# A routed layer's results: gathered and summed by the next stage, or added to the tokens' rows in HBM by DMA

## The chip, the cores and the metric

The kernel runs on one core of a Trainium2 chip. The metric is the device time of one execution in microseconds (us). The engines are PE (TensorE matmul; PEld are its weight loads), DVE (VectorE), ACT (ScalarE), POOL (GpSimd) and SP (SyncE, which here only issues DMAs). Each runs its own instructions in order and waits on semaphores for the others. A DMA is issued by an engine's queue and carried out by 16 DMA engines that all queues share.

## The reference

Four layers follow each other on 4096 tokens of 256 float32 numbers, each as `x = x + norm(layer(norm(x)))`: a windowed attention, a routed layer of experts, a second (linear, causal) attention, and a gated recurrence. The change is about the hand-over from the second to the third. The routed layer is

```python
scores = softmax(xt @ gate_w.T)                  # 8 experts
topk_w, topk_i = top_k(scores, 2)                # 2 of them for each token
comb = zeros((T, 8)).at[arange(T)[:, None], topk_i].add(topk_w)
for e in range(8):
    y = y + comb[:, e:e+1] * ((silu(xt @ w1[e]) * (xt @ w3[e])) @ w2[e])   # 256 -> 704 -> 256
y = y + (silu(x @ sw1) * (x @ sw3)) @ sw2        # shared expert, 256 -> 384 -> 256
```

and what follows is `x = x + norm(y)`, then `norm(x)` into the second attention.

## The kernel before

The tokens are 32 tiles of 128 rows, or 16 units of two tiles; a tile of x has the tokens on the 128 partitions. All arithmetic is float32.

**Stage A (0 to about 350 us): first attention, routing, most of the shared expert.** Units pass through a pipeline written out by hand: `ORDER_A` lists pieces with a lag each, and every engine executes its part in that order. When a unit is through, its normed rows lie in the SBUF tile `xrow`. `rank` computes both experts of each token, their weights (`wts`) and a slot for each copy; `send` (L835) scatters every tile of `xrow` twice, by indirect DMA from POOL, to the slots in the HBM tensor `xg_d`, which has one region for each expert. `zeros` (L862) first fills the ends of the regions with zeros (8 DMAs from SP). The last eight sends wait for these fills. The shared expert's result of units 0 to 12 goes to the HBM tensor `ysh_d`.

**Stage B (about 358 to 877 us): experts.** The rows of `xg_d` are handled in 32 blocks of 256 rows and 4 blocks of 128 (which expert a block belongs to is computed at run time; 4 more blocks stand in a branch that runs only if needed). For each block: `x_rows` (L1184, SP) loads its rows two blocks ahead, `x_cols` transposes them, `up` does the two wide products (L1211), `angle_piece` computes a part of the third layer's rotation table on DVE (into `xrow`, whose rows have been sent), and `down` of the block before (L1248, L1255) does the product back to 256 columns. `down` copies its result from PSUM to `yo` (DVE, L1258) and SP stores it at the block's place in the HBM tensor `yg_d` (L1260). Weights of the next block (2 MB) are loaded by SP meanwhile. `place_results` computes for each token where in `yg_d` its two results lie (`yslots`).

**The passage.** After the branch (L1331) SP loads the second attention's weights (`second_weights`, L1031 to L1046), and PE does the shared expert of units 13 to 15 (`shared`, L1131 and L1144), whose results SP stores to `ysh_d` (L1155), and a small product of gate weights (`gate_product`, L1351 and L1356).

**Stage C (to about 1250 us): second attention.** Again a pipeline by hand, `ORDER_C`, over 16 units; a pair `("s0", 0)` is the piece `s0` with a lag of 0 periods. What a unit passes through first is what the change is about:

```python
fy   # SP: y = the unit's rows of ysh_d (shared result); the tile k_y has 3 buffers
g0..g3  # POOL: indirect DMA, rows of yg_d by yslots -> k_g (first and second expert, two tiles)   L334
s0, s1  # DVE: y += wts * k_g, four times a unit                                                 L348
bo_st, bo_pw, bo_nr, bo_ap, bo_ad   # norm of y (DVE, POOL, DVE, ACT), then x += y on POOL (L361)
cn_st, cn_pw, cn_nr, cn_ap          # norm of x, into y again
xt, xc, qk, sq, vz, v, z, rk, rq, tk, tq, ck, cq, pe, et, ps, pn, ...    # the attention itself
```

`_st` are the statistics, `_pw` the power of -1/2 on POOL (L301), `_nr` the shift on DVE (L307), `_ap` the application on ACT (L314). In the trace: `c_xt` is the transpose of the normed unit (xt), `c_pqk` and `c_pvz` the projections, `c_sq` ACT's silu of them, `c_kn` the rotation on POOL, `c_qr` on DVE, `c_pe` the products of keys and queries, `c_et` their masking on DVE, `c_pn` the products with the values, `c_tk` the transpose of the keys. `c_tk`, `c_xt` and the projections share two PSUM buffers, which ACT's copies free; the piece v frees that of `c_pvz`.

**Stage D (to the end): recurrence**, two steps over 8 pairs of units. The change leaves it as it is.

Of the kernel before, what the change touches and what calls it, by code (L numbers as in the profile page):

```python
# [16 lines left out]
P = 128  # L17
D = 256
NT = 32
NU = 16  # L20
NBLK = 8
E = 8
# [47 lines left out]
    ("z1", 2), ("v1", 2), ("cn_st", 1), ("tk1", 2), ("os1", 3), ("co_st", 4), ("g3", 0),  # L70
    ("cq1", 2), ("pn0", 3), ("ps", 2), ("tk0", 2), ("ck1", 2), ("cn_pw", 1), ("cn_nr", 1),
    ("os0", 3), ("cn_ap", 1), ("g1", 0), ("po", 3), ("co_pw", 4), ("g2", 0), ("ck0", 2),
    ("xt", 1), ("dl", 2), ("sd", 2), ("co_nr", 4), ("xc", 1), ("gt", 3), ("pe1", 2), ("tq0", 2),
    ("g0", 0), ("co_ap", 4), ("qk0", 1), ("ci_st", 3), ("et13", 2), ("cq0", 2), ("qk1", 1),
    ("ci_pw", 3), ("et12", 2), ("et10", 2), ("et11", 2), ("s1", 0), ("sq0", 1), ("s0", 0),
# [63 lines left out]
def kernel(  # L139
# [122 lines left out]
    xg_d = dram.tile([NS, D], F32, name="xg_d")  # L262
    yg_d = dram.tile([NL * BS + NM * SS, D], F32, name="yg_d")
    ysh_d = dram.tile([NT * P, D], F32, name="ysh_d")
# [3 lines left out]
    wts = [const.tile([P, NT], F32, name=f"wt{i}") for i in range(2)]  # L268
    slots = [const.tile([P, NT], I32, name=f"slot{i}") for i in range(2)]
    yslots = [const.tile([P, NT], I32, name=f"yslot{i}") for i in range(2)]  # L270
# [8 lines left out]

# [50 lines left out]
    @piece(0, 1, 2, 3)  # L330
    def g(u, n):
        t, i = n // 2, n % 2
        rows = kb.tile([P, D], F32, name=f"k_g{u}_{n}", tag="k_g", bufs=6)
        nc.gpsimd.indirect_dma_start(  # L334
            out=rows,
            out_offset=None,
            in_=yg_d[:, :],
            in_offset=bass.IndirectOffsetOnAxis(
                ap=yslots[i][:, 2 * u + t : 2 * u + t + 1], axis=0
            ),  # L340
        )
        S2[u]["g", n] = rows

    @piece(0, 1)
    def s(u, t):
        y = S2[u]["y"]
        for i in range(2):
            nc.vector.scalar_tensor_tensor(  # L348
                y[:, t, :], S2[u]["g", 2 * t + i], wts[i][:, 2 * u + t : 2 * u + t + 1],
                y[:, t, :], ALU.mult, ALU.add,  # L350
            )

# [6 lines left out]
    def bo_ad(u):  # L359
# [5 lines left out]

    xrow = const.tile([P, NT, D], F32, name="xrow")
    table = [
        xrow[:, 2 * j : 2 * j + 2, :].rearrange("p a b -> p (a b)") for j in range(NT // 2)
    ]
# [7 lines left out]
    moves = xtp.tile([P, 3, E], F32, name="rt_moves")  # L377
# [3 lines left out]
    row0 = const.tile([P, NB], I32, name="row0")  # L381
    n_small = const.tile([P, 1], I32, name="n_small")
# [4 lines left out]
    with ExitStack() as ph:  # L387
# [30 lines left out]
        def rows_of(u):  # L418
            return xrow[:, 2 * u : 2 * u + 2, :]
# [287 lines left out]
        zero = wp.tile([P, D], F32, name="zero")  # L707
        apart = wp.tile([P, 1], F32, name="apart")

        def later_constants():  # L710
            for f in range(4):
                nc.sync.dma_start(
                    out=th_d[f], in_=theta.rearrange("(i s d) f -> f s i d", i=4, s=2)[f, 0]
                )
            for vb in vbds[1:]:
                nc.gpsimd.memset(vb, 0.0)
            nc.gpsimd.memset(zero, 0.0)
            nc.sync.dma_start(
                out=xg_d[E * REG : NS, :].rearrange("(p r) d -> p r d", p=P),
                in_=zero.unsqueeze(1).to_broadcast([P, BS // P, D]),  # L720
            )
            r0 = NL * BS + NS_ALWAYS * SS
            nc.sync.dma_start(
                out=yg_d[r0:, :].rearrange("(t p) d -> p t d", p=P),
                in_=zero.unsqueeze(1).to_broadcast([P, NM - NS_ALWAYS, D]),
            )
            for dst, step, base in ((prio, -1, E), (region, REG, 0), (bidx, 1, 0)):
                nc.gpsimd.iota(
                    dst, pattern=[[step, dst.shape[1]]], base=base, channel_multiplier=0,
                    allow_small_or_imprecise_dtypes=True,  # L730
                )

            nc.gpsimd.memset(before, 1.0)
            nc.gpsimd.affine_select(
                out=before, in_=before, compare_op=ALU.is_ge, fill=0.0, base=-1,
                pattern=[[1, P]], channel_multiplier=-1,
            )
            nc.gpsimd.memset(ones, 1.0)

            nc.gpsimd.memset(seen, 0.0)  # L740
# [4 lines left out]
        def rank(g):  # L745
# [32 lines left out]
            def best(src, m, eq, nm):  # L778
                nc.vector.tensor_reduce(m, src, AX.X, ALU.max)
                nc.vector.tensor_tensor(eq, src, wide(m), ALU.is_equal)  # L780
                nc.vector.tensor_tensor(eq, eq, per_tile(prio), ALU.mult)
                q = col(f"rt_q{nm}")
                nc.vector.tensor_reduce(q, eq, AX.X, ALU.max)
                nc.vector.tensor_tensor(eq, eq, wide(q), ALU.is_equal)

            one, two = (pick[:, ts, :] for pick in picks)
            best(sc, wts[0][:, ts], one, "a")
# [3 lines left out]
            best(rest, wts[1][:, ts], two, "b")  # L791
# [41 lines left out]
        def send(t, i):  # L833

            dma = nc.gpsimd.indirect_dma_start(  # L835
                out=xg_d[:, :],
                out_offset=bass.IndirectOffsetOnAxis(ap=slots[i][:, t : t + 1], axis=0),
                in_=xrow[:, t, :],
                in_offset=None,
            )  # L840
            sent_to_rows(dma, "dispatch" if t < 2 * NZ else "last")
# [6 lines left out]
        def zeros():  # L848
# [7 lines left out]
            for e in range(E):  # L856
# [7 lines left out]
                    in_=zero.unsqueeze(1).to_broadcast([P, rows // P, D]),  # L864
# [3 lines left out]
        def blocks():  # L868
# [48 lines left out]
            nc.vector.tensor_copy(owner[:, 0:NL], of[:, 0:NL])  # L917
            yield
# [41 lines left out]
            for k, dst in ((0, row0), (1, owner)):  # L960
# [5 lines left out]
            yield  # L966


            to_big, to_few = moves[:, 0, :], moves[:, 1, :]
            nc.vector.tensor_copy(moves[:, 2, :], start)  # L970
            nc.vector.tensor_tensor(to_big, end, big, ALU.subtract)
            nc.vector.scalar_tensor_tensor(
                to_big, to_big, float(BS), region, ALU.mult, ALU.subtract
            )
            nc.vector.tensor_tensor(to_few, few_end, few, ALU.subtract)
            nc.vector.tensor_scalar(to_few, to_few, extra, float(SS), ALU.add, ALU.mult)
            nc.vector.tensor_scalar(to_few, to_few, float(NL * BS), None, ALU.add)
            nc.vector.tensor_tensor(to_few, to_few, start, ALU.subtract)
            nc.vector.tensor_tensor(to_few, to_few, to_big, ALU.subtract)
# [101 lines left out]
    with ExitStack() as ph:  # L1081
# [15 lines left out]
        def angle_piece(i):  # L1097
# [20 lines left out]
            if i % 8 == 7:  # L1118
                done = xrow[:, i - 7 : i + 1, :]
                nc.scalar.activation(done, done, AF.Sin)  # L1120
# [3 lines left out]
        def shared_part(u, c, H):  # L1124
# [16 lines left out]
            for t in range(2):  # L1141
# [6 lines left out]
                y = kb.tile([P, D], F32, name=f"k_sh{u}_{t}", tag="k_g", bufs=6)  # L1148
# [3 lines left out]
        def shared_out(u, H):  # L1152
            for t in range(2):
                r0 = (2 * u + t) * P
                nc.sync.dma_start(out=ysh_d[r0 : r0 + P, :], in_=H[3, t])  # L1155

        def place_results():

            own = yp.tile([P, NT, E], F32, name="rt_mine")
            for i, pick in enumerate(picks):  # L1160
                got = yp.tile([P, 3, NT], F32, name=f"rt_got{i}")
                for k in range(3):
                    nc.vector.tensor_tensor(
                        own, pick, moves[:, k, :].unsqueeze(1).to_broadcast([P, NT, E]),
                        ALU.mult,
                    )
                    nc.vector.tensor_reduce(got[:, k, :], own, AX.X, ALU.add)
                nc.vector.tensor_tensor(got[:, 2, :], sfs[i], got[:, 2, :], ALU.is_ge)
                nc.vector.tensor_tensor(got[:, 2, :], got[:, 2, :], got[:, 1, :], ALU.mult)
                nc.vector.tensor_tensor(got[:, 0, :], got[:, 0, :], got[:, 2, :], ALU.add)  # L1170
                nc.vector.tensor_tensor(yslots[i], got[:, 0, :], sfs[i], ALU.add)
# [9 lines left out]
        def x_rows(b, nt, at=None):  # L1181
            at = row_of(b) if at is None else at
            xg = hp.tile([P, 2, D], F32, name=f"xg{b}", tag="row", bufs=6)
# [57 lines left out]
        def down(b, nt, wb, hs):  # L1241
# [14 lines left out]
            yo = hp.tile([P, 2, D], F32, name=f"yo{b}", tag="row", bufs=6)  # L1256
            for t in range(nt):
                nc.vector.tensor_copy(yo[:, t, :], pds[t])  # L1258
            r0 = b * BS if b < NL else NL * BS + (b - NL) * SS
            nc.sync.dma_start(  # L1260
                out=yg_d[r0 : r0 + nt * P, :].rearrange("(t p) d -> p t d", p=P),
                in_=yo[:, 0:nt, :],
            )
# [32 lines left out]
        for i in range(len(line)):  # L1296
# [17 lines left out]
            if i == 32:  # L1314
                place_results()
# [4 lines left out]
            pending = (*line[i], wbs[i], hs)  # L1320
# [10 lines left out]
        with tc.If(used > NS_ALWAYS):  # L1331
            for b in range(NL + NS_ALWAYS, NB):
                ev = expert_of(b)
                wa, wb = load_up(b, ev, wa_s), load_down(b, ev, wb_s)
                down(b, 1, wb, up(b, 1, wa, x_cols(b, 1, x_rows(b, 1))))
# [33 lines left out]
        until("g3")  # L1369
        wl, wm, kview = second_weights()  # L1370
        for c in range(4):
            shared(0, c)
        until("bo_st")
# [33 lines left out]
    with ExitStack() as ph:  # L1407
# [254 lines left out]
        def spare(i):  # L1662
            return xrow[:, 2 * i : 2 * i + 2, :]
# [314 lines left out]
```

## Time and profile before

| | us |
|---|---|
| median of 3 runs | 1445.25 (1445.15 to 1445.68) |
| the profiled execution: its own time | 1430.9 |
| its span, from the first to the last instruction | 1428.7 |
| PE busy / PEld busy | 1358.0 / 1106.0 |
| DVE / ACT / POOL busy | 914.4 / 584.1 / 518.0 |
| mean granted TensorE clock | 0.985 |
| gathers k_g on POOL, x64 | 63.7 (996 ns each) |
| weighted sums k_y on DVE, x64 | 57.6 (918 ns each) |

Busy time counts an engine's instructions; matmuls are pipelined and their ends modelled, so a busy PE is not PE at its peak. "PEclk" is the clock granted to TensorE as a share of the full one. In a row of the timeline the brackets say how long the engine sat idle before and what released it, inferred from semaphores. All durations used below come from the one profiled execution, whose time is 14.35 us under the median of the runs.

### The profile page before, as it was taken

What the parts mean: (1) busy time and instruction counts of PE and PEld (TensorE: products, weight loads), DVE (VectorE), ACT (ScalarE), POOL (GpSimd) and SP (SyncE); (2) the same over time, 40 slices, a digit from 0 to 9 for tenths busy, and PEclk for the clock granted to TensorE, in tenths of its full rate; (3) what the DMA queues carried; (4) which work ended last, traced back from release to release, by engine and by line L of the source; (5) the groups of instructions that cost most, each with busy time, mean ns of one, the idle gap of its engine ahead of it and who ended that gap; (6) DMA issues with size and microseconds to landing.
All of it is one profiled execution on the core that took longest, in us unless ns stands there. A gap on an engine that the chain in (4) does not pass through costs nothing. (4 is left out here: it accounts for less than half of the span.)

```text
span 1428.7 us, 27868 instructions
## 1 busy us (share of the span) xinstructions
PE 1358.0 (95%) x10550; PEld 1106.0 (77%) x10550; DVE 914.4 (64%) x2552; ACT 584.1 (41%) x1292; POOL 518.0 (36%) x663
## 2 busy tenths in 40 slices
PE   6999999997999999999999999899999999999996
PEld 5888888875788888888888887566666666788885
DVE  6879789877445454554454542489888898535435
ACT  5776666642221222221222221344545455344443
POOL 3435666656000000000000001468788877324333
PEclk9999999998999999999999999999999999899998
DMA  8000111118554756475656465411111110000001
GB/s 203 9 9 24 45 35 46 61 38 284 182 198 155 229 174 209 152 229 164 207 187 208 162 198 138 150 32 38 46 46 45 29 33 16 2 1 29 16 31 44
DMA packets 122553, 146.60 MB, mean 103 GB/s; under 512 B 27168, under 2 KB 99632, under 8 KB 122416
## 3 DMA queue, kind: packets, MB, share of 16 engines
q1 hardware_dynamic: 115456, 126.94, 28.2%
q0 software_dynamic: 6144, 16.79, 3.8%
q8 instruction: 85, 1.39, 0.4%
q10 hardware_dynamic: 816, 1.06, 0.2%
q14 instruction: 52, 0.43, 0.1%
HBM read 113.03 MB, written 31.72 MB: 101 GB/s over the span
## 5 line engine op out<-in xcount | busy, mean ns | idle before, releaser
L1211 PE MATMUL pg<-xgT,wa 128*128 128x256 f32 (+1 forms) x1440 | 306.2, 372 | 1.9 <-ACT xgT L1200 1.8
L1211 PEld LDWEIGHTS pg<-xgT,wa 128*128 128x128 f32 x1440 | 260.0, 191 | 46.4 <-issue 11.3
L334 POOL DMA_INDIRECT k_g<-yg_d,yslot x64 | 63.7, 996 | 540.1 <-SPq L1331 526.3
L1218 DVE TENSOR_TENSOR h<-sg,pg 128x256 f32<-128x256 f32 (+1 forms) x180 | 72.9, 406 | 218.3 <-ACT sg L1216 218.3
L1216 ACT ACTIVATE sg<-pg 128x256 f32<-128x256 f32 (+1 forms) x180 | 66.7, 371 | 355.6 <-PE pg L1211 355.6
L1248 PE MATMUL pd<-wb,h 128*128 128x256 f32 x680 | 152.8, 379 | 0.0
L1248 PEld LDWEIGHTS pd<-wb,h 128*128 128x128 f32 x680 | 126.4, 190 | 16.0 <-issue 0.3
L547 POOL TENSOR_TENSOR a_pn<-a_p,a_ri 128x512 f32<-128x512 f32 x64 | 66.7, 1045 | 79.5 <-DVE a_ri L541 48.4
L1543 DVE TENSOR_TENSOR c_et<-c_pe,causal 128x512 f32<-128x512 f32 x128 | 79.2, 679 | 1.9 <-PE c_pe L1533 1.9
L835 POOL DMA_INDIRECT xg_d<-xrow,slot x64 | 65.0, 1015 | 21.1 <-issue 9.4
L656 PE MATMUL a_sh<-xnT,was 128*128 128x256 f32 x288 | 70.8, 390 | 0.0
L1810 PE MATMUL d_pg<-d_xT,wl 128*128 128x256 f32 x288 | 70.2, 379 | 0.0
L1436 PE MATMUL c_pvz<-wl,c_xT 128*128 128x512 f32 x128 | 61.5, 604 | 0.0
L656 PEld LDWEIGHTS a_sh<-xnT,was 128*128 128x128 f32 x288 | 55.1, 195 | 8.3
L1810 PEld LDWEIGHTS d_pg<-d_xT,wl 128*128 128x128 f32 x288 | 54.6, 190 | 7.6 <-ACT d_gt L1816 0.2
L348 DVE SCALAR_TENSOR_TENSOR k_y<-k_g,wt,k_y 128x256 f32<-128x256 f32 x64 | 57.6, 918 | 3.4 <-DMA k_g<-yg_d,yslot 2.3
L1436 PE MATMUL c_pqk<-wl,c_xT 128*128 128x512 f32 x128 | 57.9, 594 | 1.4 <-ACT c_qT L1514 0.7
L520 DVE TENSOR_REDUCE a_mx<-a_s 128x8 f32<-128x512 f32 x64 | 42.7, 683 | 13.5 <-PE a_s L510 12.9
L1477 POOL TENSOR_TENSOR c_kn<-c_sq,xrow 128x512 f32<-128x512 f32 x32 | 44.7, 1396 | 17.6 <-ACT c_sq L1449 17.0
L1607 PE MATMUL c_pn<-c_et,c_v 128*32 128x128 f32 x1024 | 46.8, 277 | 2.5 <-DVE c_et L1543 0.9
L1607 PEld LDWEIGHTS c_pn<-c_et,c_v 128*32 128x32 f32 x1024 | 31.0, 109 | 21.1 <-issue 14.1
L1533 PEld LDWEIGHTS c_pe<-c_qT,c_kT 32*128 32x128 f32 x1024 | 33.3, 191 | 15.1 <-issue 12.4
(320 smaller groups left out, 2834.5 us busy)
## 6 DMA issues: line engine op xcount, KB each, us to landing
wa<-in_w_dram SPq DMA_DIRECT2D x36, 704.0 KB, 5.3
wa<-in_w_dram SPq DMA_DIRECT2D x36, 640.0 KB
wb<-in_w_dram SPq DMA_DIRECT2D x36, 640.0 KB, 4.7
xg<-xg_d SPq DMA_DIRECT2D x32, 256.0 KB, 6.0
yg_d<-yo SPq DMA_DIRECT2D x32, 256.0 KB, 2.2
xg_d<-zero SPq DMA_DIRECT2D x8, 640.0 KB, 10.4
wb<-in_w_dram SPq DMA_DIRECT2D x72, 64.0 KB, 4.3
x<-in_x_dram SPq DMA_DIRECT2D x16, 256.0 KB, 5.6
```

The lines of the kernel that those rows point to most:

```text
L334: nc.gpsimd.indirect_dma_start(out=rows, out_offset=None, in_=yg_d[:, :], in_offset=bass.IndirectOffsetOnAxis(ap=yslots[i][:, 2 * u + t : ...
L547: nc.gpsimd.tensor_tensor(to, S[u].pop(("p", g)), S[u].pop(("ri", g)).unsqueeze(2).to_broadcast([P, 8, 64]), ALU.mult,)
L656: nc.tensor.matmul(to[:, i, :], ws_up[:, k, col0 : col0 + P], turned(b)[:, k, :], start=(k == 0), stop=(k == 1),)
L835: dma = nc.gpsimd.indirect_dma_start(out=xg_d[:, :], out_offset=bass.IndirectOffsetOnAxis(ap=slots[i][:, t : t + 1], axis=0), in_=xrow[:, ...
L1211: nc.tensor.matmul(pg[:, i, 0:n], wa[:, k, col0 : col0 + P], xt[:, k, 0:n], start=(k == 0), stop=(k == 1),)
L1216: nc.scalar.activation(sg[:, 0:n], pg[:, 0, 0:n], AF.Silu)
L1218: nc.vector.tensor_tensor(h[:, 0:n], sg[:, 0:n], pg[:, 1, 0:n], ALU.mult)
L1248: nc.tensor.matmul(pds[t], hs[c][:, t * P : (t + 1) * P], wb[:, c, :], start=(c == 0), stop=False,)
L1436: nc.tensor.matmul(pq, S2[u]["xT"][:, k, t * P : (t + 1) * P], w[:, k, :], start=(k == 0), stop=(k == 1),)
L1543: nc.vector.tensor_tensor(masked, S2[u]["pe", t][i], causal.unsqueeze(1).to_broadcast([P, 4, P]), ALU.mult,)
L1607: nc.tensor.matmul(out_t[32 * c : 32 * c + 32, h, :], lhs, rhs, start=(step == 0), stop=(step == last),)
L1810: nc.tensor.matmul(pg[:, m, :], a, r, start=(i == 0), stop=(i == len(prods) - 1))
```

## The change

The rows in `xg_d` become 260 numbers wide: 256 of the token, its two weights, a number that tells its first expert, and the index of its row (as an integer). `xrow` holds them in that width, `best` writes weights and the expert's number there directly, and two iota instructions write the row indices (rows of zeros point at a spare tile at the end of `ysh_d`). `down` computes each row's weight for the block's expert from them with three small DVE operations, scales the result by it where it leaves PSUM, and adds it, tile by tile, to the rows of `ysh_d` by an indirect DMA with an add, from POOL. Such a DMA names all of `ysh_d` as its target, so each waits for the one before. The pieces g and s, `yg_d`, `yslots`, `place_results` and the last part of `blocks` (`rt_moves`) are gone. `ysh_d` is set to zero for units 13 to 15, and their shared results are added by DMA from POOL instead of stored by SP. Order of instructions: on SP the first two loads of y come after `second_weights`, and no stores of `yo` are left; on POOL the adds of the shared results stand between the pieces of the first units (those of unit 14 after bo_pw and before bo_ad of the first); PE's order does not change.

```diff
+XW = D + 4
...
-    ("z1", 2), ("v1", 2), ("cn_st", 1), ("tk1", 2), ("os1", 3), ("co_st", 4), ("g3", 0),
+    ("z1", 2), ("v1", 2), ("cn_st", 1), ("tk1", 2), ("os1", 3), ("co_st", 4), 
...   # likewise g0, g1, g2, s0 and s1 taken out of ORDER_C, nothing else moved
-    xg_d = dram.tile([NS, D], F32, name="xg_d")
-    yg_d = dram.tile([NL * BS + NM * SS, D], F32, name="yg_d")
-    ysh_d = dram.tile([NT * P, D], F32, name="ysh_d")
+    xg_d = dram.tile([NS, XW], F32, name="xg_d")
+    ysh_d = dram.tile([(NT + 1) * P, D], F32, name="ysh_d")
...
-    xrow = const.tile([P, NT, D], F32, name="xrow")
+    xrow = const.tile([P, NT * XW], F32, name="xrow")
+    sent = xrow.rearrange("p (t c) -> p t c", c=XW)
+    table = [xrow[:, 2 * D * j : 2 * D * (j + 1)] for j in range(NT // 2)]
...
+            nc.gpsimd.iota(
+                zero[:, D + 3 : XW].bitcast(I32), pattern=[[0, 1]], base=NT * P,
+                channel_multiplier=1,
+            )
+            nc.gpsimd.iota(
+                sent[:, :, D + 3].bitcast(I32), pattern=[[P, NT]], base=0, channel_multiplier=1
+            )
...
             nc.sync.dma_start(
-                out=yg_d[r0:, :].rearrange("(t p) d -> p t d", p=P),
-                in_=zero.unsqueeze(1).to_broadcast([P, NM - NS_ALWAYS, D]),
+                out=ysh_d[NSD * 256 :, :].rearrange("(t p) d -> p t d", p=P),
+                in_=zero[:, 0:D].unsqueeze(1).to_broadcast([P, NT + 1 - 2 * NSD, D]),
             )
...
-            best(sc, wts[0][:, ts], one, "a")
+            best(sc, sent[:, ts, D], one, sent[:, ts, D + 2])
...
-            best(rest, wts[1][:, ts], two, "b")
+            best(rest, sent[:, ts, D + 1], two, col("rt_q"))
...
-                in_=xrow[:, t, :],
+                in_=sent[:, t, :],
...
-                    in_=zero.unsqueeze(1).to_broadcast([P, rows // P, D]),
+                    in_=zero.unsqueeze(1).to_broadcast([P, rows // P, XW]),
...
+            nc.vector.tensor_scalar(key[:, 0:NL], of[:, 0:NL], -1.0, float(E), ALU.mult, ALU.add)
...
-                y = kb.tile([P, D], F32, name=f"k_sh{u}_{t}", tag="k_g", bufs=6)
+                y = kb.tile([P, D], F32, name=f"k_sh{u}_{t}", tag="k_g", bufs=4)
...
-                nc.sync.dma_start(out=ysh_d[r0 : r0 + P, :], in_=H[3, t])
+                if u < NSD:
+                    nc.sync.dma_start(out=rows, in_=H[3, t])
+                else:
+                    nc.gpsimd.dma_start(out=rows, in_=H[3, t], accum_op=ALU.add)
...
-            xg = hp.tile([P, 2, D], F32, name=f"xg{b}", tag="row", bufs=6)
+            xg = hp.tile([P, 2, XW], F32, name=f"xg{b}", tag="xg", bufs=5)
...
-        def down(b, nt, wb, hs):
+        def down(b, nt, wb, hs, xg):
+            ws = hp.tile([P, 3, 2], F32, name=f"rt_w{b}", tag="rt_w")
+            for i, op in enumerate((ALU.is_equal, ALU.not_equal)):
+                nc.vector.scalar_tensor_tensor(
+                    ws[:, i, 0:nt], xg[:, 0:nt, D + 2], key[:, b : b + 1], xg[:, 0:nt, D + i],
+                    op, ALU.mult,
+                )
+            nc.vector.tensor_tensor(ws[:, 2, 0:nt], ws[:, 0, 0:nt], ws[:, 1, 0:nt], ALU.add)
...
-            yo = hp.tile([P, 2, D], F32, name=f"yo{b}", tag="row", bufs=6)
             for t in range(nt):
-                nc.vector.tensor_copy(yo[:, t, :], pds[t])
-            r0 = b * BS if b < NL else NL * BS + (b - NL) * SS
-            nc.sync.dma_start(
-                out=yg_d[r0 : r0 + nt * P, :].rearrange("(t p) d -> p t d", p=P),
-                in_=yo[:, 0:nt, :],
-            )
+                yo = hp.tile([P, D], F32, name=f"yo{b}_{t}", tag="yo", bufs=5)
+                nc.vector.tensor_scalar(yo, pds[t], ws[:, 2, t : t + 1], None, ALU.mult)
+                nc.gpsimd.indirect_dma_start(
+                    out=ysh_d[:, :],
+                    out_offset=bass.IndirectOffsetOnAxis(
+                        ap=xg[:, t, D + 3 : XW].bitcast(I32), axis=0
+                    ),
+                    in_=yo,
+                    in_offset=None,
+                    compute_op=ALU.add,
+                )
...
-            if i == 32:
-                place_results()
...
-        until("g3")
         wl, wm, kview = second_weights()
+        until("bo_st")
         for c in range(4):
             shared(0, c)
-        until("bo_st")
```

## The prediction

> **What bounds the kernel now.** I first read the busy time of each engine by stage (columns: stretch; its length; busy time and count of PE, PEld, DVE, ACT, POOL; granted clock; DMA share; GB/s).
>
> ```profile
> 320.00:358.00 38.00, 27.40 (x115) 21.56 (x115) 27.98 (x138) 7.99 (x17) 23.05 (x43) 0.87 0.82 267
> 358.00:877.00 519.00, 517.42 (x2532) 438.43 (x2532) 250.26 (x688) 121.37 (x324) 0.00 (x0) 1.00 0.58 188
> 877.00:911.00 34.00, 28.98 (x118) 23.25 (x118) 11.07 (x33) 6.23 (x15) 10.60 (x12) 0.90 0.51 118
> 924.00:1204.00 280.00, 263.37 (x3042) 177.60 (x3042) 247.94 (x584) 137.46 (x290) 217.88 (x242) 1.00 0.14 39
> ```
>
> The experts (358 to 877) are bound by PE: POOL does nothing there and DVE half. The second attention (924 to 1204) has DVE, POOL and PE all near full, so the sums say little; the waits must. Its c_xt starts lie 20.07 us apart, one period per unit. This is the timeline of one period, by engine (start, length, [idle before, releaser]):
>
> ```profile
> 1047.46 3.91 DVE L348 SCALAR_TENSOR_TENSOR k_y<-k_g,wt,k_y 128x256 f32<-128x256 f32 x4
> 1052.61 0.17 DVE L296 TENSOR_SCALAR ve_bo<-mv_bo 128x2 f32<-128x2 f32 x1
> ...
> 1049.30 1.28 POOL L1477 TENSOR_TENSOR c_kn<-c_sq,xrow 128x512 f32<-128x512 f32 x1 [0.22 <-ACT c_sq L1449]
> 1052.86 1.07 POOL L301 TENSOR_TENSOR rs_bo<-ve_bo,nhalf 128x2 f32<-128x2 f32 x1 [2.29 <-DVE ve_bo L296]
> ...
> 1054.69 1.10 ACT L314 ACTIVATE k_y<-k_y,nr_bo,rs_bo 128x256 f32<-128x256 f32 x2 [2.12 <-DVE nr_bo L307]
> 1055.95 0.35 ACT L1461 COPY c_v<-c_pvz 128x256 f32<-128x256 f32 x1
> ...
> 1056.40 0.63 PE L1500 MATMUL c_tk<-ident,c_kn 128*128 128x128 f32 x4 [1.05 <-POOL c_z L1643]
> ```
>
> The weighted sums (3.91) delay bo's statistics; POOL's rs_bo waits 2.29 for them, ACT's bo_ap waits behind that, c_v comes after bo_ap on ACT, and c_tk needs the PSUM buffer that c_v frees at 1056.30: PE idles 1.05. (The profile names POOL c_z, but that had long started; c_v ends 0.1 before c_tk.) c_et, behind the same sums, is late too: the second c_pn group takes 1.97 where the first takes 1.45. So 1.57 us of each 20.07 is lost through these sums; 18.50 is PE's own work.
>
> **Removed from the second attention.** 64 gathers of about 1.0 us on POOL and 64 sums on DVE (918 ns mean, 0.98 in a full period): per period DVE falls from 17.8 to 13.9, POOL from 15.6 to 11.6. What is late next? I walk the period from c_pe = 0 (1043.39) at the durations of the rows: c_pqk ends 5.03, c_sq 5.7, c_kn 7.1, rs_bo 8.2, nr_bo 8.4, c_qr 9.1, four c_et 11.6; the second c_pn group would start at 13.57 less 1.05, 12.5. c_v ends 10.7, c_tk wants it at 11.9. Everything is in time, the tightest by 0.9, so PE sets the period at 18.5. Eleven periods of 20.07 give 17.3. Of the others, the 19.63 one gives 1.1; the last (20.39, with another 1.05 where c_xt waits for c_kT) 2.6; the second (19.15) 1.1; the first, where one gather stood before rs_cn on the path, 1.2. Sum 23.3.
>
> **Added to the experts.** 68 accumulating DMAs, two per two-tile block (the stores of yo lie 15.08 apart). Each waits on POOL until the one before has landed, since all write ysh_d; behind it on POOL stand only its successors. No such DMA is in the trace. Rows nearest to it:
>
> ```profile
> xg_d<-zero SPq DMA_DIRECT2D x8, 640.0 KB, 10.4
> yg_d<-yo SPq DMA_DIRECT2D x32, 256.0 KB, 2.2
> xg_d<-xrow,slot POOLq DMA_INDIRECT x64, 2.5
> k_g<-yg_d,yslot POOLq DMA_INDIRECT x64, 3.3
> ```
>
> The last column is us to landing. Bounds 2.2 and 10.8 (the slowest zero fill). A scatter and a gather one after the other are 5.8; I take 4.5, nearest to the scatter. Two are 9 of 15.08: hidden. It cannot gain either, as PE idles 0.07 us in 475. The same cover hides three tiny DVE operations (0.17 each) per block, a scaled copy for a plain one (0.42), and buffers held longer. Rows of 1040 for 1024 bytes in the block loads are hidden too (issued two blocks ahead), as are two iotas (POOL idles 9.82 before 23.57) and the larger early zero fill. place_results and rt_moves leave DVE where it is not waited for. Cost 0, and 0.5 at most if DVE's cover went.
>
> **Start of the experts.** Here the wider rows lie on the path:
>
> ```profile
> 342.33 0.96 POOL L835 DMA_INDIRECT xg_d<-xrow,slot  x1 [7.86 <-DVE rt_ends L887]
> ...
> 356.50 1.11 PE L1196 MATMUL xgt<-ident,xg 128*128 128x128 f32 x4 [4.59 <-DMA xg<-xg_d]
> ```
>
> The last eight sends wait 7.86 for the zero fills (issued 320.8 to 331.1, landing 10.4 later; the DVE work named had finished), and PE waits for the block load behind the sends: delays here count one to one. The eight fills are 5.24 MB, 15.5 us at the 338 GB/s of that stretch. With 1.6% more bytes that is +0.25; at the worst yield per DMA share in the trace (231 GB/s, where 64-byte pieces move) +7.2. I take +2, near the low end because the pieces stay near 1 KB. The Trainium skill, "DMA: Bandwidth & Descriptors", section "How a descriptor splits into AXI transactions", speaks against the change: a piece that does not start on a 256-byte boundary pays for bytes below its start; by that a 1040-byte row averages 36.5 beats instead of 32, an estimate from the page of +2.2, and the gain of the sum would be 0.2 smaller. No run so far shows such rows.
>
> **The passage between the stages.**
>
> ```profile
> 892.42 0.43 SPq L1046 DMA_DIRECT2D wl<-in_bo_dram  x1
> 894.08 1.09 ACT L314 ACTIVATE k_y<-k_y,nr_bo,rs_bo 128x256 f32<-128x256 f32 x2 [3.55 <-DMA wl<-in_gamma_dram]
> 895.74 2.07 PE L1356 MATMUL g<-wl 16*128 16x256 f32 x4 [1.79 <-ACT wl L1353]
> 910.41 0.60 PE L1421 MATMUL c_xt<-ident,k_y 128*128 128x128 f32 x4
> ```
>
> Today the first load of y is issued at 372.45, deep in the experts, and unit 0's statistics start at 891.67, after its sums. In the new instruction order that load stands on SP behind the eleven loads of the second weights, and must wait for the last accumulation. SP resumes when the load of the shared down weights lands (882.29); it no longer waits for the last yo, so 0.85 sooner, and the eleven end at 892.0. With 3.1 to land, as the gamma load beside it, y is there at 895.1: 3.4 later. Accumulations: the last three start at 874.5 and end 3 x 4.5 later, at 888, before 892; cover is gone above 5.8 each. POOL's branch waits for them, but its next work is due at 896.4. The gate product's ACT copy stands behind bo_ap, so PE's g moves to 899.3. Then POOL's bo_ad, at 894.75 today, stands behind two new adding stores of unit 14, which wait for PE (906.5); bo_ad ends 909.1, cn_ap 912.8, and behind cn_ap on ACT and DVE the last shared unit: c_xt at 916.0, 5.6 late. Bounds +3.4 (the load alone) and +20.4 (each accumulation 10.8: y 14.8 later still). A gain is excluded, since y now comes after the moment at which the sums ended. I keep 5.6, as 4.5 hides the accumulations.
>
> **Sum.** -23.3 + 5.6 + 2.0 = -15.7. The profiled execution took 1430.9 (span 1428.7 and 2.2 around it) and would take 1415.2. The median of the runs, 1445.25, lies 14.35 above it; taking that as constant, 1429.5. About 0.2% (2.9 us) can be told from no change.
>
> **Rivals.**
> - Accumulations bound the experts (slower). One mechanism: the wait of each on the one before, on POOL. It decides from a mean landing of 7.54 (two in 15.08). At 8 it adds 0.92 x 32 = 29 and 6.4 in the passage: -15.7 + 36 = +20, 1465; at 10.8, 209 + 15, about 1653. For it: landings of 10.4 exist, and the adds meet the weight loads. Against: 2.5 and 3.3 for 128 rows, DMA share 0.58. Chance 0.18, all slower.
> - The passage eats more: adds between 5.8 and 7.5 delay y by up to 5, and the zero fill costs up to 7.2 instead of 2: 5 + 5 = 10 less, 1439.5. Chance 0.15.
> - Another chain takes the period: the walk's 0.9 goes if c_kn takes its 1.50 and nr_bo its 0.68, rows of today. At 0.7 a period over 12, 8.4 less: 1438. For it: these durations grow when DVE and POOL overlap; against: there are fewer overlaps. Chance 0.12.
>
> **How the numbers follow.** The main case has 0.55 and 1424 to 1436 (zero fill 0.25 to 5, passage 3.4 to 8). The range 1421 to 1443 adds the second and third rivals and leaves out the first. Faster by over 0.2%: 0.55 + 0.12 + 0.10 = 0.77; within 0.2%: 0.05 of the two middle rivals; slower: 0.18.
>
> **What would show it.** Right: c_xt starts 18.5 apart with no idle before c_tk; adds landing under 5.8; yo at 15.08 spacing and PE full from 360 to 877; first c_xt about 8 later on the clock (2 + 5.6). Wrong: PE idle in the experts with DVE's yo waiting for DMA, or periods above 19.

## The result, and the profile after

The changed kernel takes 1424.64 us (median of 4 runs, 1423.53 to 1425.94) where the kernel before takes 1445.20 beside it: a ratio of 0.9859, 95% interval 0.9842 to 0.9876, or 20.6 us less. The forecast was 1429.5, 15.75 less than the 1445.25 it started from. A second timing gave 1422.69 against 1444.62 (0.9859, 0.9839 to 0.9878).

The profiled execution of the changed kernel took 1424.26, span 1422.5, so it lies at its own median. The execution of before that was shown ahead of the prediction did not; more on that below. First the busy times by stage, after (stretch, length, then busy time and count of PE, PEld, DVE, ACT, POOL, granted clock, DMA share, GB/s). The rows answer to the four of before: start of the experts, experts, passage, second attention.

```profile
331.00:370.00 39.00, 29.13 (x110) 22.63 (x108) 26.05 (x125) 7.83 (x17) 22.88 (x43) 0.81 0.83 263
370.00:889.00 519.00, 517.40 (x2532) 438.97 (x2532) 264.10 (x780) 121.54 (x324) 102.55 (x66) 0.99 0.64 188
889.00:928.00 39.00, 29.17 (x118) 23.49 (x117) 9.10 (x27) 6.12 (x15) 10.05 (x12) 0.87 0.55 98
941.00:1197.00 256.00, 255.23 (x3042) 176.16 (x3043) 194.16 (x529) 139.19 (x290) 159.07 (x187) 1.00 0.05 14
```

PE carries the same number of instructions in the experts (2532) in the same 519 us, although POOL now works there for 102.55 us. In the second attention PE is busy for 255.23 of 256, where it had 263.37 of 280. The two stretches at the experts' ends became longer at about the same number of PE instructions (110 for 115, and 118 both times).

One period of the second attention after, PE's and ACT's lines at the place where PE idled 1.05 us before:

```profile
1041.70 1.10 ACT L313 ACTIVATE k_y<-k_y,nr_bo,rs_bo 128x256 f32<-128x256 f32 x2 [0.51 <-DVE nr_bo L306]
1042.70 0.37 ACT L1440 ACTIVATE c_z<-c_pvz 128x256 f32<-128x256 f32 x1
1042.96 0.35 ACT L1430 COPY c_v<-c_pvz 128x256 f32<-128x256 f32 x1
...
1044.41 0.60 PE L1469 MATMUL c_tk<-ident,c_kn 128*128 128x128 f32 x4
```

c_v is done at 1043.31, 1.1 us before c_tk, which no longer waits. The c_xt starts lie 18.32 us apart (20.07 before).

The adding DMAs in the experts (POOL, two blocks), and the wait of the last sends:

```profile
560.09 1.55 POOL L1226 DMA_INDIRECT ysh_d<-yo,xg  x1 [6.17 <-DVE yo L1225]
567.15 1.55 POOL L1226 DMA_INDIRECT ysh_d<-yo,xg  x1 [5.50 <-DVE h L1177]
575.17 1.55 POOL L1226 DMA_INDIRECT ysh_d<-yo,xg  x1 [6.47 <-DVE yo L1225]
582.17 1.55 POOL L1226 DMA_INDIRECT ysh_d<-yo,xg  x1 [5.45 <-DVE h L1177]
```
```profile
354.52 0.96 POOL L816 DMA_INDIRECT xg_d<-xrow,slot  x1 [9.75 <-DMA xg_d<-zero]
...
368.68 1.10 PE L1155 MATMUL xgt<-ident,xg 128*128 128x128 f32 x4 [4.18 <-DMA xg<-xg_d]
```

Each holds POOL for 1.55 us, and the second of a block starts 7.0 to 7.1 us after the first, since it waits until that has landed (DVE's h is named, but is no input of it; the median of the 32 two-tile blocks is 7.3). The first of the next block waits for yo, so the second has landed by then. The sends' wait for the zero fills is 9.75 where it was 7.86.

The passage, all engines:

```profile
898.05 1.55 POOL L1226 DMA_INDIRECT ysh_d<-yo,xg  x1 [4.49 <-issue]
...
900.98 0.43 SPq L1017 DMA_DIRECT2D wl<-in_bo_dram  x1
...
903.27 0.89 SPq L324 DMA_DIRECT2D k_y<-ysh_d  x2
...
907.49 0.43 DVE L292 BATCH_NORM_STATS2 st_bo<-k_y 128x6 f32<-128x256 f32 x1 [5.95 <-DMA k_y<-ysh_d]
...
909.90 1.09 ACT L313 ACTIVATE k_y<-k_y,nr_bo,rs_bo 128x256 f32<-128x256 f32 x2 [7.09 <-DVE nr_bo L306]
...
911.56 2.07 PE L1326 MATMUL g<-wl 16*128 16x256 f32 x4 [7.22 <-ACT wl L1323]
913.56 5.17 PE L1115 MATMUL spd<-wbs,sh 128*128 128x256 f32 x12
...
919.49 0.84 POOL L1130 DMA_DIRECT2D ysh_d<-k_sh  x1 [1.35 <-DVE k_sh L1120]
920.07 1.71 POOL L337 TENSOR_TENSOR x<-x,k_y 128x256 f32<-128x256 f32 x2
...
927.87 0.60 PE L1390 MATMUL c_xt<-ident,k_y 128*128 128x128 f32 x4
```

("SPq" is SP's queue issuing a DMA.) SP has issued the last of the second weights at 901.4 and the load of y at 903.27. PE waits 7.22 us for one small ACT copy that stands behind bo_ap in ACT's order, and POOL's bo_ad (920.07) stands behind the adding stores of unit 14.

### The profile page after: what moved, and what is told of

Read it like the earlier page. It is cut to its first block, busy times and chain, and to the rows that moved or that the text cites. A ratio compares the mean times of both kernels' runs of the same rounds, so it can differ in the third digit from the quotient of the medians.

```text
span 1422.5 us, 27920 instructions
## 1 busy us (share of the span) xinstructions
PE 1360.3 (96%) x10550; PEld 1111.6 (78%) x10550; DVE 865.9 (61%) x2570; ACT 585.4 (41%) x1292; POOL 560.2 (39%) x675
## 5 line engine op out<-in xcount | busy, mean ns | idle before, releaser
L1170 PEld LDWEIGHTS pg<-xgT,wa 128*128 128x128 f32 x1440 | 260.5, 191 | 46.1 <-issue 11.3
L1226 POOL DMA_INDIRECT ysh_d<-yo,xg x68 | 105.7, 1554 | 425.4 <-DVE yo L1225 222.1
L1446 POOL TENSOR_TENSOR c_kn<-c_sq,xrow 128x512 f32<-128x512 f32 x32 | 48.9, 1528 | 21.1 <-ACT c_sq L1418 21.1
L502 DVE TENSOR_TENSOR a_p<-a_s,a_mx 128x512 f32<-128x512 f32 x64 | 43.2, 675 | 0.8
L1789 POOL TENSOR_TENSOR d_gt<-d_gt,d_gt 128x512 f32<-128x512 f32 x14 | 18.5, 1320 | 63.4 <-ACT d_gt L1785 58.9
L515 DVE TENSOR_REDUCE a_sm<-a_p 128x8 f32<-128x512 f32 x64 | 43.1, 674 | 0.0
```

Of the source, the lines that this page charges most:

```text
L1170: nc.tensor.matmul(pg[:, i, 0:n], wa[:, k, col0 : col0 + P], xt[:, k, 0:n], start=(k == 0), stop=(k == 1),)
L1226: nc.gpsimd.indirect_dma_start(out=ysh_d[:, :], out_offset=bass.IndirectOffsetOnAxis(ap=xg[:, t, D + 3 : XW].bitcast(I32), axis=0), in_=yo ...
```

## Experiments

All times are medians, timed in three rounds beside the kernel before; the ratio to it stands with its interval. The experiments ran on three chips, on which the kernel before takes 1442.15, 1444.62 and 1445.54, so times are compared within a round.

**1. The kernel before, again (twice).** No edit.

> The kernel before, unchanged. Its profiled execution took 1430.9 us, its timed runs 1445.25, while the profiled execution of the changed kernel (1424.26) lies at that kernel's own median (1424.64). Theory 1: executions of one program differ in TensorE stalls put down to issue. The profile after has some 10 us of them in the first attention (before a_py and a_s), the profile before none. Then a new profile of before has a span near 1443, with the same issue idle and the eight zero fills issued near 331 instead of 320.8. Theory 2: the 14.35 us are a constant of this kernel, not seen inside its span: a new profile is again near 1429 while the timed runs stay at 1445.

> The kernel before, unchanged, a third profile. Theory 1 (the first profile of before was the rare one): zero fills issued at 327 to 329, issue idle of PE's weight loads of 9 to 12 us in the first attention, c_xt period 20.3, span 1437 to 1444. Theory 2 (executions of both kinds are common): zero fills near 321, period 20.07, span near 1429.

Times 1441.31 (ratio 0.9997, 0.9988 to 1.0007) and 1445.80 (0.9997, 0.9983 to 1.0011), spans of the profiled executions 1438.2 and 1444.5. Waits of PE's weight loads in 200 to 300 us, the first profile of before and then the third:

```profile
PEld a_s L510 <- issue: 0.7, 4, 0.2
PEld a_xt L427 <- issue: 0.3, 2, 0.2
PEld a_py L578 <- issue: 0.3, 1, 0.3
```
```profile
PEld a_py L578 <- issue: 5.7, 12, 0.6
PEld a_s L510 <- issue: 1.5, 5, 0.5
PEld a_xt L427 <- issue: 0.5, 3, 0.2
```

Theory 1 holds, though its figures don't all (the second profile's span and fills came earlier than expected, the third's later). The first profile was of an execution that lacks idle time which the later ones have: in those, PE's weight loads sit idle before a_py and a_s, products of the first attention, and wait for nothing that the profile shows. The zero fills start at 327.32 and 332.35 in the later profiles, against 320.79; all twelve profiles after the first have them between 327 and 333. It also had a c_xt period of 20.07 where both later ones have 20.30. The stages, like with like (us; pg is the PSUM tile of the product that `up` starts with, pd that of `down`; c_xt is counted by starts):

| stretch | forecast of the change | before: first; second; third | after: first; second | means, after less second and third of before |
|---|---|---|---|---|
| start to the first of eight zero fills | 0 | 320.8; 327.3; 332.4 | 331.1; 328.8 | +0.1 |
| to the first pg | +2.0 | 37.6; 36.7; 37.5 | 39.4; 41.2 | +3.3 |
| to the last pd | 0 | 517.9; 517.9; 518.2 | 518.1; 517.3 | -0.4 |
| to the first c_xt | +5.6 | 34.2; 34.7; 34.7 | 39.3; 38.7 | +4.3 |
| to the last c_xt | -23.3 | 293.4; 296.6; 296.7 | 268.9; 268.9 | -27.7 |
| to the end | 0 | 225.0; 225.0; 225.2 | 225.7; 222.5 | -1.0 |
| sum | -15.7 | | | -21.4 |

The sum agrees with the timings (-20.6 and -21.9).

**2. The sums alone, the gathers alone.**

```
before_no_sums:     ORDER_C without ("s0", 0), ("s1", 0)
before_no_gathers:  ORDER_C without ("g0", 0) to ("g3", 0);  s:  S2[u]["g", 2 * t + i] -> xs[u][:, t, :]
                    until("g3") -> until("s1"), ahead of second_weights()
```

> The kernel before without the 64 weighted sums (so the routed results are left out of its output); the gathers stay. Theory 1 (the sums hold DVE, bo's statistics and with them c_v and c_tk): the c_xt period falls from 20.07 to 18.3 to 18.5, the time by 23 to 26 us, to about 1420. Theory 2 (POOL's gathers set the period): it stays near 20 and the time above 1440.

> The kernel before without the 64 gathers; the sums stay and read rows of x in place of the gathered ones (so the routed results are left out of its output). Theory 1 (the sums set the period): c_xt stays 19.5 to 20.1 apart, the time above 1438. Theory 2 (the gathers on POOL set it): the period falls to 18.5, the time to about 1422.

Without sums 1411.36 (0.9785, 0.9769 to 0.9802), period 18.31; without gathers 1435.69 (0.9949, 0.9930 to 0.9968), period 20.07. First to last c_xt: 269.65 and 293.0, against 268.9 after. So the gain of the second attention is that of the sums: without them it is as short as after, gathers and all. The time fell by 30.8, more than the 23 to 26 expected, because the loss in a usual execution is 27 and the passage is 3.5 shorter as well (31.2). Without the gathers the second attention keeps the period that before itself had in its first profile (20.07, 293.4), 3.6 us below its other two. The passage is shorter there too, 30.7 us from the last pd to the first c_xt, where no gather is waited for; this takes the time below the 1438 that theory 1 had as its floor.

**3. Which chain carries the sums' loss.**

```
-    ("fy", 0), ("et02", 3), ("bo_ad", 1), ... ("z1", 2), ("v1", 2), ("cn_st", 1), ... ("bo_ap", 0), ...
+    ("fy", 0), ("z1", 2), ("v1", 2), ("bo_ap", 1), ("et02", 3), ("bo_ad", 1), ... ("cn_st", 1), ...
```

> The kernel before with one place changed in the order of the second attention: on ACT the two copies c_z and c_v of the last c_pvz stand ahead of bo_ap instead of behind it. Gathers and sums stay. Theory 1 (the forecast's chain: sums, nr_bo, bo_ap, then c_v behind it on ACT, which frees the PSUM buffer that c_tk wants): PE's idle time of 1.05 to 1.28 before c_tk goes and the c_xt period falls from 20.07 to 20.30 by 1.0 to 1.3, the time by 15 to 22. What is left to 18.32 is c_et, late behind the same sums. Theory 2 (the sums cost because DVE has 3.9 us more to do in each period, wherever c_v stands): the period stays at 20.07 to 20.30 and the time within 2 us.

1444.34 (0.9994, 0.9981 to 1.0007), period 20.29. Theory 1 falls and theory 2 holds. PE in one period of this kernel, and DVE's second set of c_et:

```profile
1068.34 2.47 DVE L1543 TENSOR_TENSOR c_et<-c_pe,causal 128x512 f32<-128x512 f32 x4
...
1068.13 0.60 PE L1500 MATMUL c_tk<-ident,c_kn 128*128 128x128 f32 x4
1069.25 0.84 PE L1607 MATMUL c_pn<-c_et,c_v 128*32 128x128 f32 x8 [0.52 <-ACT c_os L1616]
1070.27 0.41 PE L1607 MATMUL c_pn<-c_et,c_v 128*32 128x128 f32 x2 [0.18 <-DVE c_et L1543]
1070.87 0.31 PE L1607 MATMUL c_pn<-c_et,c_v 128*32 128x128 f32 x3 [0.19 <-DVE c_et L1543]
...
1072.09 2.00 PE L1556 MATMUL c_pst<-c_v,c_kn 128*128 128x64 f32 x16
```

The wait before c_tk is gone, as meant. Instead c_pn waits 0.89: 0.52 put down to ACT's c_os, which stands behind bo_ap, and 0.37 for c_et. The last c_et ends at 1070.81, and c_pst, the product behind c_pn, starts 1.28 after it (1072.09), as it does in the kernel before (1065.50 and 1066.78). So the last c_et sets PE's pace with either order. This is DVE in the second profile of before, from the first c_et of a unit to its last:

```profile
1053.34 2.48 DVE L1543 TENSOR_TENSOR c_et<-c_pe,causal 128x512 f32<-128x512 f32 x4 [0.55 <-PE c_tq L1500]
1055.74 3.49 DVE L348 SCALAR_TENSOR_TENSOR k_y<-k_g,wt,k_y 128x256 f32<-128x256 f32 x4
...
1060.54 0.69 DVE L1477 TENSOR_TENSOR c_qr<-c_sq,xrow 128x512 f32<-128x512 f32 x1
1061.82 0.68 DVE L307 SCALAR_TENSOR_TENSOR nr_bo<-mv_bo,rs_bo 128x2 f32<-128x2 f32 x1 [0.59 <-POOL rs_bo L301]
1062.43 0.68 DVE L1477 TENSOR_TENSOR c_qr<-c_sq,xrow 128x512 f32<-128x512 f32 x1
1063.03 2.47 DVE L1543 TENSOR_TENSOR c_et<-c_pe,causal 128x512 f32<-128x512 f32 x4
```

DVE is at work from 1053.34 to 1065.5 with one pause of 0.59, and PE needs both ends of it: it feeds the first c_et and waits for the last. The sums are 3.5 to 3.9 us of that chain wherever c_v stands. Counted from c_xt, the second set of c_et starts at 12.5 in this kernel and in the later profiles of before, and at 10.1 without the sums and after the change. After, DVE has room: nr_bo waits 1.82 for rs_bo and c_et still comes in time. This reading rests on the traces and on the runs without sums and with c_v first; no run keeps the sums and takes them out of c_et's way.

**4. The passage.**

```
-        until("bo_st")  shared(0, 0..3)  shared(1, 0)  until("bo_nr")  shared(1, 1)
-        until("bo_ad")  shared(1, 2)  gate_product()  shared(1, 3)  until("cn_nr") ...
+        until("bo_st")  shared(0, 0..3)  shared(1, 0..2)  gate_product()
+        until("cn_st")  shared(1, 3)  until("cn_nr") ...
```

> The changed kernel with the gate product and the up parts of unit 14 ahead of bo's statistics, and bo_ad ahead of the adding stores of unit 14. Theory 1 (the passage is lost where PE waits 7.2 us for a copy of ACT that stands behind bo_ap, and POOL's bo_ad behind stores that wait for PE): the first c_xt comes 4.5 to 7 us earlier after the last pd, the time falls to 1418 to 1420. Theory 2 (what holds the passage is the load of y behind the accumulations, 903.3 to 907.4): the first c_xt stays within 1 us and the time at 1424.6.

> The changed kernel with the gate product first, once more, on the chip of the kernel before that is timed with it. Theory 1 (its gain is the 8 to 9 us of the passage and nothing else): 30 to 33 us below before, passage 30 to 31, period 18.32. Theory 2 (part of the 30.9 of its first timing was the chip): 24 to 28 below.

(The code is shortened.) 1411.22 (0.9788, 0.9772 to 0.9804), and 1414.65 (0.9791, 0.9755 to 0.9827): 30.9 below before both times, where the changed kernel was 20.6 and 21.9 below. It beats both kernels. The first c_xt comes 30.4 and 32.1 us after the last pd, instead of 39.0 (mean of two). PE's g with the product behind it, and DVE's statistics, in its first profile:

```profile
902.13 1.13 PE L1326 MATMUL g<-wl 16*128 16x256 f32 x4 [0.55 <-ACT wl L1323]
903.18 2.86 PE L1115 MATMUL spd<-wbs,sh 128*128 128x256 f32 x12
```
```profile
904.90 0.43 DVE L292 BATCH_NORM_STATS2 st_bo<-k_y 128x6 f32<-128x256 f32 x1 [2.67 <-DMA k_y<-ysh_d]
```

y arrives 19.0 us after the last pd (885.87), as in the changed kernel (18.9), but PE does not wait for what follows from it. Theory 1 holds, with more than the 4.5 to 7 that it expected: 6.9 to 8.6 us are the passage, and the rest of the 9 to 10 lies within the scatter of the other stretches. The surplus is in the clock. In the changed kernel the granted clock is 0.50 from 908 to 918, during and behind the wait of 7.22 us; there g takes 2.07 and spd 5.17. In this run it is 1.00 from 902 to 912, and the same instructions take 1.13 and 2.86. Of the 8.8 us between the two profiles' passages, 6.7 are the wait itself and 3.3 these two products, less 1.1 that PE now waits longer before the last spd.

**5. Adding against scattering, and a third addition per block.**

```
after_scatter:      -    compute_op=ALU.add,
after_three_adds:   +    nc.gpsimd.indirect_dma_start(out=ysh_d[:, :], out_offset=<spare rows>, in_=yo, ..., compute_op=ALU.add)
```

> The changed kernel, unchanged, on the same chip as the next three. Theory 1 (stage by stage, like executions): against the second profile of before (zero fills issued 327.32, first pg 363.97, last pd 881.87, first c_xt 916.52, last c_xt 1213.16) the second attention is 24 to 28 us shorter, the passage from the last pd to the first c_xt 4.5 to 5 longer, the stretch from the zero fills to the first pg 2 to 3 longer, the experts within 0.5; the time is 18 to 22 us below before's. Theory 2 (part of the 20.6 was a difference of executions): it is 14 to 17 below.

> The changed kernel with plain scatters in place of the 68 accumulating ones (so a token's row keeps only what was written last). In the trace after, a block's second accumulation starts 7.1 us after its first while the weights stream in, 4.5 when they do not, and each holds POOL 1.55. Theory 1 (adding is what costs: the row is read and written back): scatters hold POOL 1.0 and start 3 to 5 apart beside the weight loads; the last lands before the second weights are in, y comes 1 to 3 us earlier after the last pd, the time falls by 1 to 3. Theory 2 (any row DMA waits so long behind the weight loads): they stay 6.5 to 7.5 apart and the time within 1 us.

> The changed kernel with one more accumulation per block, of the last yo onto the spare rows behind the tokens (read by nobody). Three of them by 7.1 us are 21.3, more than the 15.08 us of a block. Theory 1 (each accumulation beside the weight loads takes its 7.1, so the forecast's 4.5 was too small and the cover of two is 15.08 - 14.2 = 0.9): POOL becomes the bound of the experts, each of 32 two-tile blocks takes 20 to 21.5, and the time rises by 150 to 210. Theory 2 (4.5 is the work of one, the rest is slack that a full queue does not take): three are 13.5, hidden, and only the passage is longer by some 5 to 10.

The changed kernel took 1422.69 and the scatters 1422.91 (0.9848 of before, 0.9827 to 0.9869). POOL in the experts, with scatters:

```profile
576.97 0.96 POOL L1226 DMA_INDIRECT ysh_d<-yo,xg  x1 [7.63 <-DVE yo L1225]
581.42 0.96 POOL L1226 DMA_INDIRECT ysh_d<-yo,xg  x1 [3.49 <-DMA ysh_d<-yo,xg]
```

The repeated profile of the changed kernel has the time that theory 1 expected (21.9 below before); against the second profile of before its stretch at the start of the experts grew by 4.5, where 2 to 3 were expected. Adding costs 0.6 us more on POOL, and the second of a block follows the first after 5.1 (median) instead of 7.3; that part of theory 1 of the scatters holds. The time did not follow: y's load is issued at 903.18, right behind the second weights (902.63), and unit 0's statistics start at 910.11, 19.7 us after the last pd. In the five profiles of the changed kernel, of its new order and of the scatters the load is issued 12.8 to 15.8 us after the last pd and the statistics start 18.6 to 19.7 after it, no sooner where the issue was sooner. So a faster end of the additions gains nothing; that the transfers of the second weights, issued just before, are what holds y then is likely but not tested alone.

With a third addition the time is 1480.89 (1.0258 of before, 1.0240 to 1.0277), 58 above the changed kernel; both theories miss (150 to 210, and 5 to 10).

```profile
648.99 1.55 POOL L1228 DMA_INDIRECT ysh_d<-yo,xg  x1 [4.91 <-DVE kk L1076]
654.19 1.55 POOL L1228 DMA_INDIRECT ysh_d<-yo,xg  x1 [3.65 <-DMA ysh_d<-yo,xg]
658.19 1.55 POOL L1237 DMA_INDIRECT ysh_d<-yo,spill  x1 [2.44 <-DMA ysh_d<-yo,xg]
665.36 1.55 POOL L1228 DMA_INDIRECT ysh_d<-yo,xg  x1 [5.62 <-DVE ang L1081]
```

Now the queue of additions hardly ever empties: 104 of them start between 402.4 and 956.8, one each 5.4 us. About one of three takes some 7 and most others 4.0 to 5.9. Three are 16 us in a block of 15.08, so the experts grow by 21 and a queue of additions is left over that delays the load of y to 961.67 (passage 73.5, +34.5).

**6. The wider rows alone.**

```
before_wide:  xg_d [NS, D] -> [NS, D + 4], and with it zero, xrow, xg and the zero fills;  k_g bufs 6 -> 5
```

> The kernel before with rows of 1040 bytes in xg_d (zero fills, sends, block loads), and nothing else of the change but one buffer fewer for k_g. Theory 1 (the wider rows are what the start of the experts lost): the stretch from the first of the eight zero fills to the first pg is 1.5 to 3 us longer than the 36.65 of the second profile of before, and the time 1 to 4 us above before's. Theory 2 (what was lost there came from the order of the instructions or from the executions): the stretch stays within 0.7 of 36.65.

From the zero fills to the first pg 40.9; the six profiles with 1024-byte rows have 36.7 to 37.7, those of the changed kernel and its variants 39.2 to 41.2. The sends wait 11.08. They are released 21.1 to 21.6 us after the first zero fill in the six profiles with the narrow rows and 23.2 to 24.9 in the seven with the wide ones, so nearly all of it is lost at the fills. Theory 1 holds for this stretch, at 3 to 4 us instead of 1.5 to 3. The total, 1462.95 (1.0144, 1.0119 to 1.0168), missed its 1 to 4 and can't be used for the rows: the passage is 10 us longer (44.9; the sums wait 11.2 for a gather) and the second attention 4.5, most likely through the buffer that I took from k_g.

## Where the prediction was right and where it was not

- **Second attention, -23.3.** The step held in its sum, and was too small by 1.1 against the profile that it was made from (293.36 to 268.93): PE's own period is 18.32, not 18.50, so the eleven periods gave 19.3 instead of 17.3, while the first gave 0.3 instead of 1.2. That the errors nearly cancelled is luck. What failed is the chain: c_v behind bo_ap was named as the carrier of most of the loss (1.05 of 1.57), and experiment 3 shows that freeing it alone gains nothing. The chain that holds is the one that got the smaller part, c_et behind the sums on DVE.
- **"Taking that as constant": the offset of 14.35.** This step failed, and cost 3.3 of the 4.9 us by which the forecast was too high. The first profile's execution was about 9 us shorter before the zero fills than the other two, which the change doesn't touch, and 3.3 us shorter in the second attention. These 3.3 go when the sums go, and also when the gathers alone go (20.07), so the change took them too: the saving in a usual execution was 27.7. The 20.30 in place of 20.07 could be seen only in a second profile.
- **Start of the experts, +2.0 (0.25 to 7.2).** Mis-sized: 3.3 as the table's means, and 3 to 4 with the wider rows alone. The bytes (+0.25) don't explain it. The estimate of +2.2 from the Trainium skill, "DMA: Bandwidth & Descriptors", section "How a descriptor splits into AXI transactions", is nearer to it. But the page speaks of bytes that are fetched below a piece's start, the fills write into the wide rows, and no run separates the rows' start from their length; so the agreement confirms nothing.
- **Experts, 0.** Right, though the price behind it was mis-sized: 4.5 for each addition, where one beside the weight loads takes 7.3 and one in a free stretch 4.5. Two are below 15.08 all the same, by a smaller margin than the 6 us it was given; the sign "adds landing under 5.8" did not come. An estimate from the third addition's run: the pair costs about 7 + 4.3 = 11.3, which leaves less than one more.
- **Passage, +5.6.** Right (+4.3; +5.1 against the first profile). y was forecast 18.9 us after the last pd and came after 18.9, in part by luck: issue at 15.8 and 3.1 to land were forecast, 14.7 and 4.2 came. That the additions end 11.8 after the last pd, before the weights' loads are issued, was wrong: those were all issued by 12.8, and the load of y had to wait until 14.7 for the last addition. The rival's condition, additions of 5.8 to 7.5, was met, but not at the end, where they start 4.5, 4.5 and 6.0 apart. The two places in the order that the prediction named, PE's g behind bo_ap and bo_ad behind the adding stores, are what cost: taking both away gave 6.9 to 8.6 us, 3.3 of it (in the first of the two profiles) through the clock, which the sum did not have as a term.
- **Rivals.** Additions as the bound of the experts: not here, but from three a block on it is so, at the 5.4 us of a full queue. The passage as the larger loss: no. Another chain as the period: no, PE is busy for 255.23 of 256 us.

## What to carry to other kernels

A profile is of one execution: where it lies 1% off the median of the runs, take a second one before the difference is called constant, because part of it may sit in the very stage that is changed. An idle gap that one wait ends tells what came last, not what carries the loss; an order change that frees only that wait shows it for little. When a load moves behind a long queue, look for small instructions of other engines that stand behind its consumers: here one copy of 0.34 us held PE for 7.2. Such a wait is paid for again where the granted clock is low behind it: two products took 3.3 us longer at 0.50 than at 1.00.

## What the runs showed of the hardware that was not expected

- An adding indirect DMA of 128 rows of 1 KB holds POOL for 1.55 us, a plain one for 0.96. In a chain the adding ones start 4.0 to 4.6 us apart where they run free and about 7.3 apart at the weight loads' bursts; the plain ones 4.1 to 4.5 and 5.1.
- PE's weight loads have 10.6 to 13.6 us of idle time put down to issue in the first 320 us of all profiles but the first (3.5 there); what they wait for is open.
- The second attention of the kernel before settles in a period of 20.07 in one execution and 20.30 in others, each kept to 0.02 us over eleven units. With 20.30 DVE's first c_et and ACT's c_qT start 0.6 us later after c_xt than with 20.07 (2.8 to 2.9 against 2.2), a wait put down to PE's c_tq; without the gathers or without the sums they start at the early time. What decides it is open.
